# Four-layer cross attention, batches taken three at a time: another order of turns for the grouped-query layer, which adds into its input's tile

## The chip, the cores and the metric

The kernel runs on one core of one Trainium2 chip. The metric is the device time of one execution in microseconds. The profile is one execution taken by the hardware profiler; its engines are TensorE (PE, with weight loads shown apart as PEld), VectorE (DVE), ScalarE (ACT), GpSimd (POOL) and SyncE (SP, which here only issues DMAs).

## The reference

`x` is (4 batches, 512 queries, 256 channels); the context is (4, 1024 keys, 512 channels). Four cross-attention layers follow each other, and each one's output is the next one's input. All is float32.

```python
# layers 0, 2, 3: "masked", 16 heads of 64
q, k, v = x @ Wq, ctx @ Wk, ctx @ Wv
logits = q k^T * 64**-0.5 + col_bias      # col_bias: -20 * (1 - mask) in four chosen key columns
x = softmax(logits) v @ Wo + bo + x

# layer 1: grouped query, 16 query heads of 16, 4 key/value heads
xn = x * rsqrt(mean(x*x) + eps) * norm_w
q, k, v = xn @ wq, ctx @ wk, ctx @ wv
x = x + softmax(q k^T / 4) v @ wo
```

Batches do not depend on each other; layers of one batch do.

## The kernel before, in words

**Units.** Each layer of a batch is cut into eight units, so there are 4 x 4 x 8 = 128: 96 masked and 32 grouped. A masked unit is two heads of 64, side by side in the 128 partitions. A grouped unit is two heads as well, each in a stripe of 32 rows (16 and padding), with even and odd key blocks in the two halves of the partitions, so that four matmuls of 32 rows lie side by side; two consecutive units share one query projection and one output projection.

**Steps.** Two strings, `MASKED_TURNS` and `GROUPED_TURNS` (lines 55 to 62), say for each step which stream gives its next masked unit and which its next grouped unit; a dot is none. `order()` (line 65) pops the units. Before, stream 0 is batch 0 and then batch 2, stream 1 is batch 1 and then batch 3, and there are 104 steps: 72 with a masked unit alone, 24 with both ("attached"), and 8 with a grouped unit alone (steps 11 to 14, 28, 29, 78 and 79). The program is written out in this order by hand; each engine runs its own instructions in it.

**A step** (the loop at line 967) with a masked unit `g`, a grouped unit `lam`, the previous masked unit `g1` and the next step's grouped unit `coming`:

- `scores(g)` (line 642 on): 32 matmuls (line 652), ScalarE copies each 128x1024 tile out of PSUM (662), VectorE keeps a running maximum (666).
- The previous masked unit is attended, `attend(g1)` (684). If `lam` is there, its logits are computed again in four pairs between quarters of this (616) and ScalarE takes exponentials right out of PSUM (639).
- VectorE subtracts the maximum (749), ScalarE exponentiates (755), POOL adds up the running sums (794). These are interleaved by the due times in `events`.
- A list `fill` holds the TensorE work that needs no softmax: output projections of units attended a step earlier (840, added by VectorE at 862 or 858), query projections (548), `attend` of `lam`, keys of the masked unit two steps on (472), at the head of a grouped layer its keys (490) and RMS norm (580 to 595), then transposes of newly loaded inputs (378, 352), and values for the next step (514). Maxima of `coming` (608, logits at 616) are strewn between these by due time (line 1089).
- In a step with a grouped unit alone there are no scores, subtractions or running sums; maxima of `coming` and exponentials of `lam` alternate pair by pair (lines 1051 to 1063), with one output and one query projection in between.

**Buffers.** PSUM's eight banks are handed out by `Place`, longest free first. The states of the batches (a layer's input and the sum that becomes its output) live in four slots of one SBUF tile, `x_all`, given out and taken back by `new_state` and `drop_state`. Three contexts fit at once (`bufs=3`). The tile `stage` (one buffer) takes raw context and input as they are loaded, the norm's scratch and the rows to be stored. Keys, values, `xn` and query weights of the grouped layer have one buffer each.

**Loads.** SP's queue loads weights a few steps ahead. Raw context comes by POOL's gathers in four parts and x in a fifth, one a step, from five steps before the unit two ahead of a batch's first masked unit (lines 917 to 927). For batches 2 and 3 the fifth part is put off until the batch that gave them its stream is nearly done.

**project_out** (line 832): the first projection of a layer opens the next state. It takes a slot and writes input plus projection into it; later ones add in place. A grouped layer's input is dropped as soon as its first projection is added.

Of the kernel before, what the change touches and what calls it, by code (L numbers as in the profile page):

```python
# [17 lines left out]
B, S, C = 4, 512, 256  # L18
# [24 lines left out]
def units(b):  # L43
    out = []
    for l in range(4):
        for u in range(8):
            out.append(
                Group(l=l, b=b, u=u, p=u, r=u // 2, h=u % 2, first=u == 0, last=u == 7)
            )
    return out  # L50

MASKED_TURNS = (
    "00000000111....1111100000000..0011111111000000000000"
    "00111111111111111100000000..001111111100000011111111"
)
GROUPED_TURNS = (
    "...........00000000....11111111....................."  # L60
    ".....00000000........11111111......................."
)


def order():
    streams = [units(0) + units(2), units(1) + units(3)]
    steps = []
    for turns in zip(MASKED_TURNS, GROUPED_TURNS):
        steps.append([None if s == "." else streams[int(s)].pop(0) for s in turns])
        assert all(g is None or g.masked == (n == 0) for n, g in enumerate(steps[-1]))  # L70
    assert not any(streams)
    return steps


# [1 line left out]
def kernel(ctx: ExitStack, tc: tile.TileContext, a: dict, out: bass.AP):  # L76
# [240 lines left out]
    xs, ctx_t = {}, {}  # L317
# [3 lines left out]
    x_free, x_at = [0, 1, 2, 3], {}  # L321

    def new_state(l, b):
        x_at[l, b] = x_free.pop(0)
        xs[l, b] = x_all[:, x_at[l, b]]
        return xs[l, b]

    def drop_state(l, b):
        x_free.append(x_at[l, b])
# [246 lines left out]
    turns = []  # L576
# [255 lines left out]
    def project_out(g):  # L832
        x, acc = xs[g.l, g.b], xs.get((g.l + 1, g.b))
        opens = acc is None
        if opens:
            acc = new_state(g.l + 1, g.b)
        w = Place()
        m = w.ap
        for k in range(KC):
            nc.tensor.matmul(  # L840
                m[:, k * S : (k + 1) * S], lhsT=g.wo[:, k * P : (k + 1) * P], rhs=g.ot,
                start=True, stop=True,
            )
        y = m.rearrange("p (k q) -> p k q", q=S)

        def add_last(q):
            nc.vector.tensor_tensor(acc[:, :, q], y[:, :, q], acc[:, :, q], ALU.add)

        def add():
            if g is masked[-1]:  # L850
                for i in range(0, NI, 2):
                    add_last(slice(i * P, (i + 2) * P))
                    store(g.b, range(i, i + 2))
                left[g.b] = -1
            elif opens and g.masked:
                bo = columns[f"L{g.l}_xattn_bo"]
                for k in range(KC):
                    nc.vector.scalar_tensor_tensor(
                        acc[:, k, :], y[:, k, :], bo[:, k : k + 1], x[:, k, :], ALU.add, ALU.add
                    )  # L860
            else:
                nc.vector.tensor_tensor(acc, y, x if opens else acc, ALU.add)
            if opens and not g.masked:
                drop_state(g.l, g.b)
            w.back()

        left[g.b] -= 1
        return add

    def store(b, blocks=range(NI)):  # L870
        x = xs[4, b]
        o = t_([P, NI, C], "stage", f"out{b}_{blocks[0]}")
        w = Place()
        m = w.ap
        for n, i in enumerate(blocks):
            for k in range(KC):
                nc.tensor.transpose(
                    m[:, n * C + k * P : n * C + (k + 1) * P], x[:, k, i * P : (i + 1) * P], ident
                )
        count = len(blocks)  # L880
        (nc.vector.tensor_copy if blocks[0] else nc.scalar.copy)(
            o[:, 0:count, :], m[:, 0 : count * C].rearrange("p (i c) -> p i c", c=C)
        )
        if blocks[-1] == NI - 1:
            drop_state(4, b)
        w.back()
        nc.sync.dma_start(
            out=out[b].rearrange("(i p) c -> p i c", p=P)[:, blocks[0] : blocks[-1] + 1, :],
            in_=o[:, 0:count, :],
        )  # L890
# [3 lines left out]


    steps = order()
    masked = [g for g, _ in steps if g]
    step_of = {(g.l, g.b, g.u): n for n, both in enumerate(steps) for g in both if g}
# [3 lines left out]
    def at(n):  # L902
        return steps[n] if 0 <= n < len(steps) else (None, None)
# [14 lines left out]
    for b in range(B):  # L918
        first = next(g for g in masked if (g.b, g.l, g.u) == (b, 0, 0))
        for n, part_of in enumerate(load_parts(b, first.n == 0)):  # L920
            at_step = -1
            if first.n:
                before = masked[first.n - 2]
                at_step = step_of[before.l, before.b, before.u] - 5 + n
                if n == 4 and b > 1:
                    at_step = step_of[3, b - 2, 7] - 1
            parts.setdefault(at_step, []).append(part_of)

    def run(items):
# [37 lines left out]
    for n in range(len(steps) + 2):  # L967
        g, lam = at(n)
# [79 lines left out]
        if lam:  # L1048
            if g1:
                reciprocal_sums(g1)  # L1050
            for i in range(NT // 2):
                if g1:
                    attend(g1, range(2 * i, 2 * i + 2))
                if coming and not g:
                    pair(i)
                exponentials_pair(lam, i)
                if i == 0 and g:
                    g.mx_place.back()
                if not g:
                    if i == 1 and outs:  # L1060
                        project_out(outs.pop(0))()
                    if i == 2 and queries:
                        project_q(queries.pop(0))()
# [5 lines left out]
        elif g1 and g:  # L1069
            attend(g1)  # L1070
            if not ending:
                late.append(lambda: normalise(g1))
        elif g1:
            attend_last(g1)
            adds = [project_out(each) for each in outs]
            outs = []
            reciprocal_rows(g1.ot, g1.psum, g1.mx)
            scale_out(g1)
            for add in adds:
                add()  # L1080
# [10 lines left out]


        fill = [(1.8, lambda each=each: project_out(each)) for each in outs]
        outs = []
        of_queries = [(1.7, lambda each=each: project_q(each)) for each in queries]
# [97 lines left out]
```

## Time and profile before

| | |
|---|---|
| time, median of 3 runs (lowest to highest) | 3808.96 us (3808.76 to 3809.16) |
| the profiled execution's own time | 3809.19 us |
| its span, first to last instruction | 3807.4 us |
| granted TensorE clock, mean | 0.997 |
| PE busy | 3741.1 us (98%) |
| DVE busy | 3001.7 us (79%) |
| ACT busy | 2101.8 us (55%) |
| POOL busy | 1624.5 us (43%) |
| first matmul of the masked scores | 35.0 us after the span's start |

Busy time is a share of the whole span. Matmuls are pipelined and their ends are modelled, so a busy PE need not be PE at its peak. In the views of instructions a row is: start, duration, engine, line, operation, output<-inputs, shapes, count, and in brackets the idle time before it with what ended it. In views of stretches the columns are: start and end of the stretch, its length, then busy time and count of instructions for PE, PEld, DVE, ACT and POOL (for one line's instructions, of the engines it uses), the granted clock, the DMA engines' share and GB/s.

### The profile page before, as it was taken

What the parts mean: (1) busy time and instruction counts of PE and PEld (TensorE: products, weight loads), DVE (VectorE), ACT (ScalarE), POOL (GpSimd) and SP (SyncE); (2) the same over time, 40 slices, a digit from 0 to 9 for tenths busy, and PEclk for the clock granted to TensorE, in tenths of its full rate; (3) what the DMA queues carried; (4) which work ended last, traced back from release to release, by engine and by line L of the source; (5) the groups of instructions that cost most, each with busy time, mean ns of one, the idle gap of its engine ahead of it and who ended that gap; (6) DMA issues with size and microseconds to landing.
All of it is one profiled execution on the core that took longest, in us unless ns stands there. A gap on an engine that the chain in (4) does not pass through costs nothing.

```text
span 3807.4 us, 50450 instructions
## 1 busy us (share of the span) xinstructions
PE 3741.1 (98%) x19662; PEld 1879.9 (49%) x19662; DVE 3001.7 (79%) x3928; ACT 2101.8 (55%) x2433; POOL 1624.5 (43%) x749
## 2 busy tenths in 40 slices
PE   8999999999999999999999999999999999999998
PEld 4555444554434555555545444555444355555554
DVE  6887778778877888888887887788787778888887
ACT  4555455555545555555555555555555455555554
POOL 3555113443313555555553333445332155555554
PEclk9999999999999999999999999999999999999999
DMA  2111000010000001101011010100100000000100
GB/s 67 42 31 26 12 24 18 17 33 22 19 11 23 26 26 42 37 26 31 26 25 36 27 27 18 29 26 19 28 20 23 11 25 26 25 26 26 31 24 7
DMA packets 187874, 98.71 MB, mean 26 GB/s; under 512 B 43240, under 2 KB 183528, under 8 KB 187636
## 3 DMA queue, kind: packets, MB, share of 16 engines
q1 hardware_dynamic: 182510, 82.90, 7.9%
q0 software_dynamic: 2560, 8.39, 0.8%
q10 hardware_dynamic: 2566, 4.20, 0.5%
q8 instruction: 155, 2.54, 0.3%
q14 instruction: 83, 0.68, 0.1%
HBM read 89.16 MB, written 2.10 MB: 24 GB/s over the span
## 4 chain that ended last, share of the span: by engine, by line
PE 87%; DVE 8%; ACT 2%; issue 2%; DMA 0%; POOL 0%; DVEq 0%; ACTq 0%; POOLq 0%
PE ps L514 19%; PE ps L684 19%; PE ps L472 17%; PE ps L652 13%; PE ps L616 7%; PE ps L840 5%; PE ps L548 5%; DVE ps L666 4%; ACT st L662 1%; DVE st L749 1%; DVE st L608 1%; PE ps L490 1%; PE ps L658 1%; DVE qt L634 1%; PE ps L704 0%
## 5 line engine op out<-in xcount | busy, mean ns | idle before, releaser
L794 POOL TENSOR_TENSOR st<-st 128x1024 f32<-128x1024 f32 x668 | 1579.7, 2365 | 2059.7 <-ACT st L755 2015.7
L666 DVE TENSOR_TENSOR ps<-ps,st 128x1024 f32<-128x1024 f32 x672 | 828.2, 1232 | 466.3 <-ACT st L662 407.4
L755 ACT ACTIVATE st<-st 128x1024 f32<-128x1024 f32 x768 | 783.2, 1054 | 707.1 <-DVE st L749 695.2
L749 DVE TENSOR_TENSOR st<-st,ps 128x1024 f32<-128x1024 f32 x768 | 885.0, 1212 | 3.3
L684 PE MATMUL ps<-st,v 128*64 128x512 f32 (+1 forms) x4064 | 805.7, 597 | 0.5 <-DVE st L608 0.5
L662 ACT COPY st<-ps 128x1024 f32<-128x1024 f32 x768 | 715.4, 1047 | 101.8 <-PE ps L658 81.4
L514 PEld LDWEIGHTS ps<-wv,ctx 128*128 128x128 f32 x6400 | 729.8, 192 | 73.9 <-issue 63.6
L514 PE MATMUL ps<-wv,ctx 128*128 128x128 f32 x6400 | 742.3, 276 | 0.6 <-ACT st L662 0.6
L652 PE MATMUL ps<-qt,kt 64*128 64x512 f32 x3072 | 708.3, 598 | 1.4 <-ACT qt L554 1.4
L472 PE MATMUL ps<-ctx,wk 128*128 128x512 f32 x1536 | 689.6, 598 | 2.2 <-ACT ctx L384 2.2
L684 PEld LDWEIGHTS ps<-st,v 128*64 128x64 f32 (+1 forms) x4064 | 233.5, 130 | 545.6 <-issue 480.7
L472 PEld LDWEIGHTS ps<-ctx,wk 128*128 128x128 f32 x1536 | 288.1, 191 | 389.1 <-issue 373.2
L652 PEld LDWEIGHTS ps<-qt,kt 64*128 64x128 f32 x3072 | 283.8, 186 | 326.4 <-ACT st L662 146.0
L526 ACT COPY v<-ps 128x512 f32<-128x512 f32 x200 | 117.1, 585 | 497.1 <-PE ps L514 493.2
L608 DVE TENSOR_TENSOR st<-st,ps 128x1024 f32<-128x1024 f32 x224 | 273.3, 1220 | 129.8 <-PE ps L616 61.2
L616 PE MATMUL ps<-qt,kt 32*128 32x512 f32 x2048 | 323.8, 645 | 28.1 <-DVE qt L634 16.3
L639 ACT ACTIVATE st<-ps 128x1024 f32<-128x1024 f32 x256 | 248.4, 1023 | 185.2 <-PE ps L616 156.7
L840 PE MATMUL ps<-ot,wo 128*128 128x512 f32 x448 | 217.4, 611 | 1.4 <-DVE ot L829 0.7
L616 PEld LDWEIGHTS ps<-qt,kt 32*128 32x128 f32 x2048 | 103.4, 186 | 214.1 <-issue 57.1
L548 PE MATMUL ps<-x,wq 128*128 128x512 f32 x384 | 185.6, 606 | 1.8 <-ACT x L356 1.1
L477 ACT COPY kt<-ps 128x512 f32<-128x512 f32 x192 | 109.8, 572 | 77.3 <-PE ps L472 77.0
L840 PEld LDWEIGHTS ps<-ot,wo 128*128 128x128 f32 x448 | 78.5, 189 | 135.2 <-issue 124.2
(143 smaller groups left out, 1633.2 us busy)
## 6 DMA issues: line engine op xcount, KB each, us to landing
wk<-in_L_xattn_Wk_dram SPq DMA_DIRECT2D x96, 256.0 KB
wv<-in_L_xattn_Wv_dram SPq DMA_DIRECT2D x96, 256.0 KB
wq<-in_L_xattn_Wq_dram SPq DMA_DIRECT2D x96, 128.0 KB
wo<-in_L_xattn_Wo_dram SPq DMA_DIRECT2D x96, 128.0 KB
qt<-qt ACTq DMA_DIRECT2D x32, 128.0 KB
xraw<-in_x_dram SPq DMA_DIRECT2D x3, 512.0 KB
out_dram<-out SPq DMA_DIRECT2D x3, 512.0 KB
wq<-in_L_xattn_wq_dram SPq DMA_DIRECT2D x32, 32.0 KB
```

The lines of the kernel that those rows point to most:

```text
L472: nc.tensor.matmul(m, lhsT=g.wk[:, k, :], rhs=ctx_t[g.b][:, k, n * 512 : (n + 1) * 512], start=(k == 0), stop=(k == KT - 1),)
L514: nc.tensor.matmul(m[:, t * P : (t + 1) * P], lhsT=ctx_t[g.b][:, k, (4 * n + t) * P : (4 * n + t + 1) * P], rhs=g.wv[:, k, :], start=(k == ...
L548: nc.tensor.matmul(m, lhsT=g.wq[:, k, :], rhs=x[:, k, :], start=(k == 0), stop=(k == KC - 1))
L616: nc.tensor.matmul(ws[odd].ap[:, j * S : (j + 1) * S], lhsT=g.kt[rows, i * P : (i + 1) * P], rhs=g.qt[rows, :], start=True, stop=True,)
L652: nc.tensor.matmul(m[:, j * S : (j + 1) * S], lhsT=g.kt[g.rows[j], keys], rhs=g.qt[g.rows[j], :], start=True, stop=t > 0,)
L662: nc.scalar.copy(g.st[t], m)
L666: nc.vector.tensor_tensor(top, top, g.st[t], ALU.max)
L684: nc.tensor.matmul(g.po[at, :], lhsT=g.v[:, t, rows], rhs=g.st[t][:, j * S : (j + 1) * S], start=(t == first), stop=(t == last),)
L749: nc.vector.tensor_tensor(g.st[t], g.st[t], g.mb, ALU.subtract)
L755: nc.scalar.activation(st, st, AF.Exp)
L794: nc.gpsimd.tensor_tensor(g.acc, g.st[0] if t == 1 else g.acc, g.st[t], ALU.add)
L840: nc.tensor.matmul(m[:, k * S : (k + 1) * S], lhsT=g.wo[:, k * P : (k + 1) * P], rhs=g.ot, start=True, stop=True,)
```

## The change

Each batch becomes a stream of its own. The strings are new: 96 steps, each with a masked unit, and all 32 grouped units attached: batch 0's in steps 11 to 18, batch 1's in 21 to 28, batch 2's in 31 to 38, batch 3's in 67 to 74. Batches 0, 1 and 2 start their first layers one after the other (steps 0, 8, 16) and are in progress together; batch 3 starts at step 56, after batch 0 has ended at 47. The first projection of a grouped layer no longer opens a slot: the sum goes into the input's own tile, which becomes the next state under its own slot, and nothing is dropped. The exception for the fifth part of batches 2 and 3 is gone: x is loaded in the step after the last context part.

```diff
 MASKED_TURNS = (
-    "00000000111....1111100000000..0011111111000000000000"
-    "00111111111111111100000000..001111111100000011111111"
+    "000000001111111122222222000000001111111100000000"
+    "222222223333333311111111222233333333222233333333"
 )
 GROUPED_TURNS = (
-    "...........00000000....11111111....................."
-    ".....00000000........11111111......................."
+    "...........00000000..11111111..22222222........."
+    "...................33333333....................."
 )
...
-    streams = [units(0) + units(2), units(1) + units(3)]
+    batches = [units(b) for b in range(B)]
...
     def project_out(g):
         x, acc = xs[g.l, g.b], xs.get((g.l + 1, g.b))
         opens = acc is None
-        if opens:
+        if opens and g.masked:
             acc = new_state(g.l + 1, g.b)
+        elif opens:
+
+            acc = xs[g.l + 1, g.b] = x
+            x_at[g.l + 1, g.b] = x_at[g.l, g.b]
...
-            if opens and not g.masked:
-                drop_state(g.l, g.b)
...
                 at_step = step_of[before.l, before.b, before.u] - 5 + n
-                if n == 4 and b > 1:
-                    at_step = step_of[3, b - 2, 7] - 1
```

More of the change, by code (lines that the diff above doesn't have):

```diff
@@ L55 @@
 MASKED_TURNS = (
-    "00000000111....1111100000000..0011111111000000000000"
-    "00111111111111111100000000..001111111100000011111111"
+    "000000001111111122222222000000001111111100000000"
+    "222222223333333311111111222233333333222233333333"
 )
 GROUPED_TURNS = (
-    "...........00000000....11111111....................."
-    ".....00000000........11111111......................."
+    "...........00000000..11111111..22222222........."
+    "...................33333333....................."
 )
 def order():
-    streams = [units(0) + units(2), units(1) + units(3)]
+    batches = [units(b) for b in range(B)]
     steps = []
     for turns in zip(MASKED_TURNS, GROUPED_TURNS):
-        steps.append([None if s == "." else streams[int(s)].pop(0) for s in turns])
+        steps.append([None if s == "." else batches[int(s)].pop(0) for s in turns])
         assert all(g is None or g.masked == (n == 0) for n, g in enumerate(steps[-1]))
-    assert not any(streams)
+    assert not any(batches)
     return steps
```

## The prediction

> **What bounds the kernel now.** I read the page's busy shares first, then the chain that ended last, then cut the trace into steps and read stretches of it, and last the order of time inside one stretch.
>
> ```profile
> span 3807.4 us, 50450 instructions
> ...
> PE 3741.1 (98%) x19662; PEld 1879.9 (49%) x19662; DVE 3001.7 (79%) x3928; ACT 2101.8 (55%) x2433; POOL 1624.5 (43%) x749
> ...
> PE 87%; DVE 8%; ACT 2%; issue 2%; DMA 0%; POOL 0%; DVEq 0%; ACTq 0%; POOLq 0%
> ```
>
> TensorE is busy nearly all the time and carries 87% of the chain; 8% lies on VectorE. DMA is nowhere on it. The change leaves TensorE's work as it is, so the question is where TensorE loses time now, and 98% cannot tell: the ends of matmuls are modelled.
>
> So I cut by steps. Each masked step opens with the 32 score matmuls of line 652; the first of them marks its start. A step with a masked group alone lasts 31.94 us, again and again; with eight transposes in it, 32.82. In the next view the columns are start and end, length, and the busy time and count of each engine. The rows are: eight plain steps; three steps with transposes; the stretches that hold the grouped layer of batch 0 (steps 9 to 19), 1 (21 to 30), 2 (55 to 65) and 3 (71 to 80); the four grouped-only steps 11 to 14 alone; one attached step (62).
>
> ```profile
> 3286.85:3542.38 255.53, 255.53 (x1233) 136.54 (x1232) 210.97 (x272) 144.09 (x168) 132.74 (x57) 1.00 0.09 25
> 136.78:235.24 98.46, 98.46 (x489) 53.69 (x488) 79.39 (x102) 56.81 (x66) 53.65 (x26) 1.00 0.14 41
> 331.02:727.74 396.72, 383.92 (x2243) 177.70 (x2242) 297.39 (x384) 212.84 (x245) 120.69 (x61) 0.99 0.08 21
> 759.68:1187.65 427.97, 416.31 (x2397) 191.35 (x2396) 321.08 (x414) 231.46 (x267) 140.06 (x69) 0.99 0.09 21
> 1959.55:2477.10 517.55, 511.43 (x2909) 242.46 (x2908) 402.27 (x521) 291.31 (x335) 194.51 (x97) 1.00 0.11 28
> 2636.80:3063.20 426.40, 414.26 (x2398) 189.96 (x2397) 321.06 (x414) 231.48 (x267) 140.05 (x69) 1.00 0.09 21
> 418.90:507.24 88.34, 81.89 (x573) 28.85 (x572) 58.00 (x78) 41.15 (x46) 0.88 (x3) 1.00 0.08 18
> 2301.77:2350.11 48.34, 47.92 (x285) 21.42 (x284) 37.96 (x48) 28.16 (x32) 16.58 (x7) 1.00 0.06 17
> ```
>
> TensorE never idles in a plain step (255.53 busy of 255.53). In the grouped stretches it idles 12.8, 11.7, 6.1 and 12.1 us. The low one is batch 2, the only one whose eight grouped units all ride on masked steps. The four lone units alone idle 6.45 us, and POOL has 0.88 us of work there.
>
> The same stretches for the grouped logits (line 616, 512 matmuls in each):
>
> ```profile
> 331.02:727.74 396.72, 84.49 (x512) 28.36 (x512) 0.99 0.08 21
> 759.68:1187.65 427.97, 82.62 (x512) 26.69 (x512) 0.99 0.09 21
> 1959.55:2477.10 517.55, 75.78 (x512) 22.89 (x512) 1.00 0.11 28
> 2636.80:3063.20 426.40, 80.87 (x512) 25.51 (x512) 1.00 0.09 21
> ```
>
> One and the same work takes 5.1 to 8.7 us longer where part of it runs alone: part of a wait looks busy. The order of time inside a lone step shows which wait:
>
> ```profile
> 434.51 1.99 PE L616 MATMUL ps<-qt,kt 32*128 32x512 f32 x12
> 435.74 2.57 DVE L608 TENSOR_TENSOR st<-st,ps 128x1024 f32<-128x1024 f32 x2 [1.77 <-PE ps L616]
> ...
> 437.01 1.13 PE L616 MATMUL ps<-qt,kt 32*128 32x512 f32 x4 [0.52 <-DVE st L608]
> ```
>
> Maxima and exponentials of a lone unit take their PSUM places from each other; TensorE waits for VectorE to empty one (0.52 us here), while VectorE waited 1.77 us for TensorE. In attached steps eight such matmuls stand between attends or key projections (1.14 us each time at 2284.4, 2287.4 and 2290.4), and the emptying is covered.
>
> **What the Trainium skill says.** "TensorEngine Tiling (Array Packing)", PSUM Bottleneck: tiling speeds up the matmuls but not the emptying of PSUM, which may become the bottleneck. The trace agrees: eight packed matmuls, 1.14 us, make two 128x1024 tiles that VectorE takes 1.22 us each to fold in. "Perfetto Trace Analysis", Optimization Strategy: where the contended engine changes over time, interleaving the regimes may help. Plain steps (all TensorE) and lone steps (a ring of waits) are two such regimes. The same page, Identifying the Most-Contended Engine, says matmul busy time is no measure of distance from the roofline; the 84.49 against 75.78 agrees, so I sum lengths of steps, not busy times.
>
> **The change, part by part.**
>
> *Order of turns.* 104 steps become 96; 96 masked and 32 grouped units stay. Lone grouped steps go from 8 to 0, attached from 24 to 32. Of each stretch I take its length less 31.94 for each masked step in it, which is the price of one batch's grouped layer:
>
> - batch 0: 396.72 - 7 x 31.94 = 173.14 (four lone steps)
> - batch 1: 427.97 - 8 x 31.94 = 172.45 (two lone)
> - batch 3: 426.40 - 8 x 31.94 = 170.88 (two lone)
> - batch 2: 517.55 - 11 x 31.94 = 166.21; it also holds five eight-transpose parts of batch 3's load and a store's eight, at 32.82 - 31.94 = 0.88 each, 5.28: 160.93 (none lone)
>
> Before: 173.14 + 172.45 + 160.93 + 170.88 = 677.40. After: 4 x 160.93 = 643.72. Gain 33.7 us. Two lone steps cost nearly as much as four, so the loss belongs to the stretch with its way in and out: step 30, attached but with no masked group to attend, takes 39.30 us for 216 matmuls where step 64 takes 43.32 for 252, although the 36 missing (32 attends at 7.09, four projections at 1.7) are worth 8.8. All three stretches go, way in and out included.
>
> Cross-check: idle above batch 2's, 6.7 + 5.6 + 6.0 = 18.3, plus line 616 above batch 2's, 8.7 + 6.8 + 5.1 = 20.6, is 38.9, an upper end; it forgets that in attached steps other lines swell a little. I take the lengths.
>
> *What the new order moves past each other.* Batches 0 and 3 repeat batch 2's pattern with a four-step lead from the layer before. Batches 1 and 2 start two steps after the one before them ends, so steps 19 and 29 hold both a tail (one more output projection: 33.66 - 31.94 = 1.72) and a head (keys and norm: 42.68 - 31.94 = 10.74). The trace has no such step. Both are TensorE work and I add them: 44.40, nothing extra. Its cost lies between -1.7 each (the head's norm waits 1.73 us for ScalarE's square, which 1.72 us of matmuls ahead of it could cover) and +3.6 each: VectorE does 0.72 + 0.25 + 0.71 + 0.69 for the tail's sums and 1.22 for the second add ahead of subtractions, and the square stands behind the exponentials that wait for those. I take 0. Single buffers (keys, values, xn, query weights of the grouped layer) have their last reader in step 18 or before and are refilled from 19 on: cover one step.
>
> *Loads.* Parts of batch 2 fall in steps 9 to 13 and of batch 3 in 49 to 53, the same count as before, 0.88 each. x now comes right behind the context on SP's queue, ahead of that step's weights. Batch 1's did so up to step 5, steps 2 to 5 at 32.82 each: nothing. Store of batch 0 falls in step 49 and takes the staging tile between two context parts; POOL's gather of step 50 waits for that store. The last half store is issued at 3804.2 and all ends at 3807.4, so a whole one lands within some 6 us, and POOL is busy with running sums until 6.2 us into a step anyway (1953.58 + 12.11 against 1959.55). Running sums queue behind it, with about 10 us before they start. I take 0; uncovered it is 6 us, once.
>
> *In place.* The first add of a grouped layer writes onto its input. Same instruction and shape as the others of line 862 (1217 ns). Its other readers, the square and the norm's two multiplications in step 9, end four steps earlier: no wait, 0. It frees the fourth slot, which three batches at a time need.
>
> Sum: 3807.40 - 33.68 = 3773.72 span; 3809.19 - 3807.40 = 1.79 around it; 3775.5. The profiled execution is 0.2 above the median of the runs, so 3775.3.
>
> **Rivals.**
>
> 1. *As summed*, 3775.3; own range 3771 to 3780. For it: batch 2 is a measured copy of the end state. Chance 0.70.
> 2. *Head on tail costs*: steps 19 and 29 lose 3.6 each, 7, and the store's 6 us is not covered: 3788 at most, 3783 likely. Against it: VectorE has 42 us of work in a 50.8 us attached step, 29.5 in a head step. 0.12.
> 3. *More gain*: the cross-check's 38.9, or the cover of both norm waits (3.5): 3770. 0.10.
> 4. *No change*: the loss belongs to the layer's own chain and comes back spread over attached steps, 33.7 / 8 = 4.2 us on each of eight newly attached: 3809. Against it: batch 2's steps are 16.4 to 18.9 above a plain one, all eight. 0.05.
> 5. *Slower*: POOL. In the lone steps of batch 0 its memset of query weights (line 434) waited 67.6 us in two waits for a projection. If such a wait moves in front of the running sums (16.6 us a step), which the next step's row sums need some 15 us in while POOL ends at 6, all beyond 9 us stalls VectorE, its subtractions, then TensorE. It decides beyond 34 us over three heads, 11 each, hence waits of 20: 3815 at 22. Against it: in batch 2's attached steps the memset waits for nothing. 0.03.
>
> **How the numbers follow.** Forecast 3775.3. The range holds 1, 3 and most of 2: 3768 to 3786. About 0.2%, 7.6 us, is what a measurement can tell: faster 0.92, same 0.05, slower 0.03.
>
> **What would show it.** Attached steps at 48 to 51 us; every grouped stretch about 161 above 31.94 per masked step; line 616 near 4 x 75.8 = 303 us where it is now 323.8; TensorE's idle down from 66 to about 48 us; steps 19 and 29 near 44.4. Wrong if a step between 19 and 31 or 49 and 51 idles on TensorE for more than 3 us, if POOL waits on line 434 inside attached steps, or if line 616 stays at 324.

## The result, and the profile after

The changed kernel takes 3774.36 us (median; 3773.92 to 3774.68) against 3808.86 us for the kernel before in the same comparison: a ratio of 0.9911, 95% interval 0.9895 to 0.9926. The forecast was 3775.3. The profiled execution took 3773.92 us.

The page of the changed kernel, its lines for span, TensorE and the chain:

```profile
span 3772.2 us, 50461 instructions
...
PE 3723.8 (99%) x19662; PEld 1860.2 (49%) x19662; DVE 3000.4 (80%) x3928; ACT 2104.1 (56%) x2433; POOL 1625.0 (43%) x749
...
PE 86%; DVE 9%; issue 2%; ACT 2%; DMA 0%; DVEq 0%; POOL 0%; ACTq 0%; POOLq 0%
```

The 19662 matmuls are the same; TensorE's idle time went from 66.3 to 48.4 us and its busy time from 3741.1 to 3723.8. Line numbers are about one higher than before up to the projection (616 is now 617, 652 is 653), and five higher at the additions.

Stretches of the changed kernel. The rows are: eight plain steps (76 to 83); steps 9 to 39 with the grouped layers of batches 0, 1 and 2; steps 65 to 75 with that of batch 3; the two steps that hold a tail and a head (19 and 29); one attached step (23). Columns as before: stretch, length, busy time and count of PE, PEld, DVE, ACT and POOL, clock, DMA share, GB/s.

```profile
3124.53:3380.07 255.54, 255.54 (x1234) 136.49 (x1233) 211.18 (x273) 144.23 (x168) 130.79 (x56) 1.00 0.09 25
329.89:1807.42 1477.53, 1459.25 (x8307) 681.69 (x8307) 1153.90 (x1493) 825.50 (x950) 531.99 (x257) 1.00 0.09 23
2611.41:3124.53 513.12, 507.12 (x2868) 238.09 (x2867) 402.33 (x521) 286.44 (x330) 186.87 (x89) 1.00 0.09 23
813.56:857.95 44.39, 42.66 (x195) 20.70 (x194) 32.98 (x44) 21.83 (x25) 16.59 (x8) 1.00 0.11 23
1293.67:1338.06 44.39, 42.66 (x195) 20.71 (x194) 32.97 (x44) 21.83 (x25) 16.60 (x8) 1.00 0.12 23
1002.89:1053.72 50.83, 50.49 (x291) 22.39 (x291) 41.93 (x56) 27.91 (x32) 16.84 (x8) 1.00 0.08 23
```

The plain step has not moved: 255.54 / 8 = 31.94. Three grouped layers cost 1477.53 - 31 x 31.94 = 487.39, less five parts of a load at 0.88, 482.99: 161.0 each. The fourth costs 513.12 - 11 x 31.94 - 0.88 (a store) = 160.90. Together 643.9 where before they cost 677.4: 33.5 us of the 35.2 by which the span is shorter. The rest is the start (first scores at 33.8 instead of 35.0 us) and the last step (45.7 us from its first score matmul to the span's end, instead of 46.4), which the change does not explain. In the traces of all fourteen kernels of this document the first scores lie between 33.7 and 35.3 us, and the last step takes 45.7 us where the granted TensorE clock falls to half once in it and 46.2 to 47.8 us where it falls twice.

The grouped logits in the same two stretches:

```profile
329.89:1807.42 1477.53, 227.01 (x1536) 68.28 (x1536) 1.00 0.09 23
2611.41:3124.53 513.12, 75.64 (x512) 22.74 (x512) 1.00 0.09 23
```

302.65 us for all four, 75.7 for each: the price that only batch 2 had before.

What TensorE still waits for in the changed kernel, its own waits, longest first (total, times, longest):

```profile
PE ps L617 <- DVE qt L635: 12.8, 32, 0.7
PE ps L588 <- ACT xn L581: 6.9, 4, 1.7
```

The first is a wait before the first pair of exponentials in each of the 32 attached steps, for the queries that VectorE lowers by the maxima (line 635, "the lowering" from here on); the second is the norm's, once in each grouped layer.

### The profile page after: what moved, and what is told of

It is laid out like the page before. It is cut to its first block, busy times and chain, and to the rows that moved or that the text cites. A ratio compares the mean times of both kernels' runs of the same rounds, so it can differ in the third digit from the quotient of the medians.

```text
span 3772.2 us, 50461 instructions
## 1 busy us (share of the span) xinstructions
PE 3723.8 (99%) x19662; PEld 1860.2 (49%) x19662; DVE 3000.4 (80%) x3928; ACT 2104.1 (56%) x2433; POOL 1625.0 (43%) x749
## 4 chain that ended last, share of the span: by engine, by line
PE 86%; DVE 9%; issue 2%; ACT 2%; DMA 0%; DVEq 0%; POOL 0%; ACTq 0%; POOLq 0%
PE ps L515 19%; PE ps L685 18%; PE ps L473 17%; PE ps L653 12%; PE ps L617 7%; DVE ps L667 6%; PE ps L845 5%; PE ps L549 5%; ACT st L663 2%; DVE st L750 1%; PE ps L491 1%; DVE qt L635 1%; PE ps L659 1%; PE ps L705 0%; PE ps L379 0%
## 5 line engine op out<-in xcount | busy, mean ns | idle before, releaser
L685 PE MATMUL ps<-st,v 128*64 128x512 f32 x4064 | 810.9, 598 | 0.0
L685 PEld LDWEIGHTS ps<-st,v 128*64 128x64 f32 x4064 | 231.2, 130 | 551.5 <-issue 491.6
L617 PE MATMUL ps<-qt,kt 32*128 32x512 f32 x2048 | 302.6, 639 | 16.1 <-DVE qt L635 12.8
L617 PEld LDWEIGHTS ps<-qt,kt 32*128 32x128 f32 x2048 | 91.0, 183 | 191.0 <-ACT st L640 52.2
```

Of the source, the lines that this page charges most:

```text
L617: nc.tensor.matmul(ws[odd].ap[:, j * S : (j + 1) * S], lhsT=g.kt[rows, i * P : (i + 1) * P], rhs=g.qt[rows, :], start=True, stop=True,)
L685: nc.tensor.matmul(g.po[at, :], lhsT=g.v[:, t, rows], rhs=g.st[t][:, j * S : (j + 1) * S], start=(t == first), stop=(t == last),)
```

## Experiments

A lone step is one with a grouped unit alone, a break is one or more of them in a row, and the way in and the way out are the steps on either side. My theory: the 33.7 us are the three stretches with lone steps; they go with the stretch and not with each lone step in it, because in a lone step VectorE and TensorE take PSUM places from each other in a ring; the shared tile costs and brings nothing. Rivals: the shared tile matters; ScalarE's exponentials are the wait; every lone step has its own price.

**1. Each part alone.** The old order with the sum in the input's tile:

```diff
# kernel before
-        if opens:
+        if opens and g.masked:
             acc = new_state(g.l + 1, g.b)
+        elif opens:
+            acc = xs[g.l + 1, g.b] = x
+            x_at[g.l + 1, g.b] = x_at[g.l, g.b]
...
-            if opens and not g.masked:
-                drop_state(g.l, g.b)
```

> The old order of turns, with the grouped layer adding into its input's tile. My theory: the same instructions in the same order, so no change: 3808.9 within 2 us, the three stretches with lone grouped steps keep their 172.5, 173.1 and 170.9 us above 31.94 per masked step. Rival (the shared tile is what brings time, or costs a wait): more than 4 us either way, and VectorE's first add of the grouped layer (line 862 of before) waits longer.

Measured 3808.92 us, 1.0001 of the kernel before (0.9992 to 1.0009). The three stretches cost 173.3, 172.5 and 170.9 above their plain steps.

The new order, with a new state for batches 0 to 2:

```diff
# changed kernel
-        if opens and g.masked:
+        moves = opens and not g.masked and g.b < 3
+        if opens and (g.masked or moves):
             acc = new_state(g.l + 1, g.b)
...
                 nc.vector.tensor_tensor(acc, y, x if opens else acc, ALU.add)
+            if moves:
+                drop_state(g.l, g.b)
```

> The new order of turns, while batches 0, 1 and 2 open a new state in the grouped layer as before (batch 3 must stay in place, four slots don't hold it otherwise). My theory: the order brings everything, 3774.4 within 2 us. Rival (the shared tile brings a part): some 3/4 of that part comes back, over 3778.

Measured 3775.17 us, 0.9912 (0.9896 to 0.9929), and the grouped stretches as long as with the whole change (487.41 and 161.78 above the plain steps). So the order brings the gain, and the shared tile has no time of its own that these runs can tell. By the program's count of states, batch 3 alone needs it: when its grouped layer gives its first sum, in step 69, batch 1 holds two of the four slots, batch 2 one and batch 3's input one. There it is a condition of the order.

**2. Whose emptying is it?** Both kernels are the one before, with a smaller operation in lone steps only.

```diff
# small_fold: maxima of `coming` when there is no masked unit
-                nc.vector.tensor_tensor(g.mx, g.mx, w.ap, ALU.max)
+                nc.vector.tensor_tensor(few(g.mx), few(g.mx), few(w.ap), ALU.max)
# small_exp: exponentials of `lam` when there is no masked unit
-            nc.scalar.activation(g.st[2 * i + odd], w.ap, AF.Exp)
+            nc.scalar.activation(few(g.st[2 * i + odd]), few(w.ap), AF.Exp)
# few: 8 of each bank's 512 columns
```

> The kernel before, where in grouped-only steps VectorE folds only 16 of the 1024 columns of a logits tile into the maximum, so that PSUM is emptied sooner (the maxima are then incomplete: that part is left out). My theory: VectorE's emptying is the wait of lone steps, so 15 to 30 us go, to 3780 to 3794, and line 616 falls from 323.8 towards 303 us. Rival (the loss belongs to ScalarE's exponentials, or to the chain from maxima to query weights): less than 6 us.

> The kernel before, where in grouped-only steps ScalarE takes exponentials of only 16 of the 1024 columns of a tile (the other exponentials are left out). My theory: VectorE is the later of the two, so less than 8 us go, 3801 or more. Rival (ScalarE's emptying is the wait): 15 to 30 us go.

Small folds: 3792.47 us (one run, and one for small exponentials), 16.3 less than the kernel before. Its four grouped stretches (batches 0 to 3, the same steps as in the prediction's view):

```profile
331.13:721.49 390.36, 379.49 (x2243) 176.73 (x2242) 268.01 (x384) 212.42 (x245) 120.64 (x61) 1.00 0.09 21
753.44:1175.62 422.18, 411.91 (x2398) 190.11 (x2397) 306.43 (x414) 231.16 (x267) 140.06 (x69) 1.00 0.09 21
1947.49:2465.06 517.57, 511.44 (x2908) 242.33 (x2907) 402.35 (x521) 291.34 (x335) 194.50 (x97) 1.00 0.11 28
2624.77:3046.59 421.82, 411.92 (x2398) 190.13 (x2397) 306.45 (x414) 231.15 (x267) 140.04 (x69) 1.00 0.09 21
```

Above the plain steps these are 166.78, 166.66, 166.23 (with its loads and store, as before) and 166.30. From batches 0, 1 and 3, 6.3 + 5.8 + 4.6 = 16.7 us have gone, and 5.9, 5.7 and 5.4 us above 160.9 remain. The same place in a lone step as the prediction showed, in order of time:

```profile
433.25 2.58 PE L619 MATMUL ps<-qt,kt 32*128 32x512 f32 x16
434.48 0.47 DVE L611 TENSOR_TENSOR st<-st,ps 128x16 f32<-128x16 f32 x2 [1.77 <-PE ps L619]
...
435.77 1.98 PE L548 MATMUL ps<-xn,wq 128*128 128x512 f32 x4
```

Sixteen matmuls stand in a row, without the 0.52 us in the middle, and the two folds take 0.47 us instead of 2.57. Small exponentials: 3808.66 us, and the stretches at 172.93, 172.47, 166.24 and 170.89, each within 0.2 us of before.

So making VectorE's folds small takes half of the loss, and making ScalarE's exponentials small in lone steps takes none of it while the folds are whole. No run makes both small; with small folds, TensorE's visible waits for ScalarE in batch 3's two lone steps come to 0.3 us. Line 616 fell by 10.6 us only, to 313.2 and not towards 303. The other half is one price for each stretch, 5.4 to 5.9 us, for four lone steps as for two. The way out holds much of it: step 80, attached but with nothing to attend between its pairs of exponentials, takes 38.08 us in the kernel before and with small folds, 3.6 more than step 64 less its 36 missing matmuls (43.32 - 8.8). What TensorE waits for there, with small folds (the third line ends at the step's first matmul):

```profile
PE ps L619 <- DVE qt L637: 2.1, 1, 2.1
PE ps L548 <- ACT st L642: 0.7, 1, 0.7
PE ps L655 <- ACT qt L554: 0.7, 1, 0.7
PE ps L619 <- ACT st L642: 0.3, 1, 0.3
```

The longest is for the lowered queries (line 637 here), 2.1 us where an attached step of the changed kernel waits some 0.4; the second and fourth are for ScalarE's exponentials of an attached step, which neither run made small.

The granted TensorE clock has a small part too. In the kernel before it is at half for 6.83 us in step 15 and again in step 30, on the way out of the first two stretches, and at full speed in step 80, on the way out of the third. The two pieces at half speed, then steps 30 and 80:

```profile
519.00:525.83 6.83, 6.83 (x28) 2.93 (x24) 4.85 (x9) 6.32 (x7) 0.00 (x0) 0.50 0.01 2
1160.71:1167.54 6.83, 6.65 (x23) 3.17 (x22) 4.91 (x9) 6.43 (x8) 0.00 (x0) 0.50 0.00 0
1148.37:1187.66 39.29, 37.04 (x216) 19.50 (x216) 22.44 (x24) 26.27 (x30) 15.11 (x7) 0.91 0.09 28
3025.12:3063.20 38.08, 34.98 (x217) 18.14 (x217) 22.44 (x24) 26.16 (x30) 15.12 (x7) 1.00 0.10 28
```

With small folds neither step has such a piece; step 30 then takes 38.08 us as well, 1.2 less, and step 15 takes 45.74 instead of 46.67. So about 2.1 of the 16.7 us came by way of the clock, which leaves 14.6 for the waits at the folds themselves. Why the clock fell in these two steps and not in step 80 is not shown. The changed kernel's clock is at full speed from its first scores to its last step.

**3. How does it grow with the number of lone steps?** Dots put into the second half of the changed kernel's masked turns, where batch 3's grouped units ride:

```diff
# changed kernel; GROUPED_TURNS lengthened to match
-    "222222223333333311111111222233333333222233333333"
+    "22222222333333331111111.1222233333333222233333333"      # lone_one
+    "22222222333333331111111..1222233333333222233333333"     # lone_two
+    "222222223333333311111....111222233333333222233333333"   # lone_four
+    "222222223333333311111.11.1222233333333222233333333"     # lone_apart
```

> The changed kernel with one grouped-only step put into batch 3's grouped layer (its fifth unit). My theory: the loss belongs to a stretch with its way in and out: about 9 us above the changed kernel, 3783. Rival (a loss for each lone step, 3.0 to 5.8 us from the stretches of before): 3778 to 3780.

> The changed kernel with two grouped-only steps, one after the other, in batch 3's grouped layer (fifth and sixth unit). Both theories: about 10 us above the changed kernel, 3784, since before had two stretches of this length at 10.0 and 11.5 us above the attached batch.

> The changed kernel with four grouped-only steps in a row in batch 3's grouped layer (third to sixth unit). My theory: 11 to 13 us above the changed kernel, 3786 to 3787.5. Rival (a loss for each lone step): 20 us, 3794.

> The changed kernel with two grouped-only steps apart from each other in batch 3's grouped layer (third and sixth unit). My theory: two stretches, so twice what one lone step costs, about 18 us above the changed kernel, 3792. Rival (a loss for each lone step): as much as two in a row, 10 us, 3784.

Times: 3794.30, 3794.95, 3794.62 and 3802.62 us, one run each, so I go by the stretch that holds the same 14 masked steps from the layer's head on. One line for each kernel, in this order: changed kernel, lone_one, lone_two, lone_four, lone_apart.

```profile
2611.41:3220.35 608.94, 602.95 (x3329) 289.27 (x3328) 481.64 (x624) 340.53 (x393) 234.67 (x109) 1.00 0.09 24
```

```profile
2612.64:3238.50 625.86, 609.78 (x3329) 293.30 (x3329) 482.17 (x624) 340.84 (x393) 234.73 (x109) 0.99 0.09 23
```

```profile
2612.39:3240.21 627.82, 609.22 (x3330) 294.27 (x3329) 482.34 (x624) 340.45 (x393) 234.60 (x109) 0.99 0.09 23
```

```profile
2611.55:3240.67 629.12, 609.28 (x3330) 297.32 (x3329) 482.76 (x624) 340.03 (x393) 234.49 (x109) 0.99 0.09 23
```

```profile
2612.70:3248.51 635.81, 613.26 (x3329) 295.41 (x3328) 482.49 (x624) 340.67 (x393) 234.59 (x109) 0.99 0.09 23
```

The work is the same, and the lengths differ by +16.9, +18.9, +20.2 and +26.9 us. One lone step costs nearly what four in a row do, so the price is for breaking the rhythm in the main. The rival's prices per lone step fit only the four: 3.0 to 5.8 us expected for one and 16.9 measured, 10 for two apart and 26.9 measured, 20 for four and 20.2 measured. But my sizes were wrong as well, each by 7 to 9 us: 9 expected for one, 10 for two, 11 to 13 for four, 18 for two apart.

Two apart would be 33.8 at twice one. To see what each break cost, I cut both kernels at the step between them. First the changed kernel, the steps with batch 3's second to fourth unit (68 to 70) and those with its fifth to eighth (71 to 74, with a store); then lone_apart, the same units with one lone step in each part and without the store:

```profile
2750.87:2898.39 147.52, 146.34 (x860) 65.20 (x859) 117.90 (x151) 84.30 (x96) 50.50 (x24) 1.00 0.08 21
2898.39:3090.87 192.48, 190.92 (x1122) 86.57 (x1121) 149.66 (x196) 111.01 (x126) 66.76 (x30) 1.00 0.08 22
2752.15:2885.49 133.34, 122.79 (x710) 52.94 (x709) 93.15 (x118) 66.56 (x75) 33.91 (x17) 0.96 0.07 17
2885.49:3054.03 168.54, 159.78 (x955) 70.34 (x954) 122.33 (x160) 91.88 (x104) 48.75 (x23) 1.00 0.06 17
```

Each part of lone_apart has one masked step less. The break at the third unit costs 133.34 - (147.52 - 31.94) = 17.8 us, that at the sixth 168.54 - (192.48 - 31.94 - 0.88) = 8.9. In the kernel before, two lone steps at the sixth and seventh unit cost 11.5 and 10.0, and four from the first unit on 12.2. So breaks that begin at the third or fifth unit cost 17 to 20 us, those at the first or sixth 9 to 12. TensorE's longest waits in lone_one from step 70 on:

```profile
PE ps L630 <- DVE mcol L730: 3.0, 1, 3.0
PE ps L617 <- DVE qt L635: 2.8, 2, 2.4
PE ps L617 <- DVE short L815: 2.1, 1, 2.1
```

All are for VectorE: on the way in for the column maxima (3.0), in the lone step for the sums of the masked unit (2.1), on the way out for the lowered queries (2.4). In lone_apart the first two are 3.0 and 2.0 at the third unit and 1.2 and 0.6 at the sixth, 3.3 us of the difference of 8.9. An odd-numbered unit comes right after a pair of units is finished, whose normalising (lines 571 to 800) stands on VectorE ahead of those sums. The clock differs too: at the third unit it is at half for 3.41 and 6.83 us, which is worth 5.1 us at most (an estimate, half of 10.24), and at the sixth it is at full speed. lone_one has the same two pieces, lone_two and lone_four two of 3.41 us. No run holds the clock still or leaves out the finished pair, so how the rest of the 8.9 us divides is not shown.

**4. Can the remaining waits be taken too?** Three kernels on top of the changed one: the lowering of the grouped queries two score tiles earlier; the norm behind the next unit's values; both.

```diff
# lower_early (also in both)
-            if t == 5:
+            if t == 3:
                 within()
# norm_late (also in both): the whole of norm(), square and matmuls
-            fill.append((1.7, norm))                 # ahead of loads and values
+            fill.append((1.7, norm))                 # behind values(masked[g.n + 1])
```

> The changed kernel with the lowering of the grouped queries after the fourth score tile of the step instead of after the sixth. In the changed kernel TensorE waits 12.8 us in all for it (line 617 for VectorE's line 635), about 0.4 in each attached step. My theory: that wait goes and nothing takes its place: 3762, 10 to 13 us less. Rival (the pair is then held up by PSUM places or by ScalarE, which empties the last score tiles until then): less than 3 us.

> The changed kernel with the norm's matmuls behind the values of the next masked unit in the head step of a grouped layer, so that ScalarE's square is done by then. TensorE waits 1.73 us there, four times. My theory: 6 to 7 us less, 3768. Rival (the norm's reciprocals come later on VectorE and hold up the next step's subtractions or its query projection): no gain, or up to 5 us more.

> Both edits on the changed kernel. If each stands for itself: the sum of the two, 3755 to 3758. Rival (they share a resource): less than the larger of the two.

All three miss. lower_early: 3808.4 us (0.9999 of the kernel before, 0.9991 to 1.0007): the whole gain of the change is lost again. norm_late: 3780.08 us, 5.7 more than the changed kernel. Both: 3812.03. TensorE's waits with the lowering early:

```profile
PE ps L653 <- DVE qt L635: 39.1, 32, 1.5
PE ps L588 <- ACT xn L581: 6.9, 4, 1.7
```

The wait for line 635 is still there, three times as long, and it is now a score tile (653) that waits. In step 23 the matmuls for the lowering start at 1017.58 us, but VectorE reaches it only at 1020.94, behind three running maxima. The lowering holds its PSUM place until then, and the seventh score tile is next in turn for that place. The 32 attached steps grew by 1.03 us on average, 33.0 in all. With the norm late, TensorE still idles 1.63 us before line 588: the square moved along with its matmuls and stands on ScalarE's queue behind the copies of the very values that were put ahead of it (the last copy starts at 370.51 us, the square at 371.00). The norm's VectorE work now comes ahead of the next step's running maxima, which in step 10 start 4.2 us into the step instead of 3.4. The steps after three of the heads grew by 0.6 to 0.8 us; step 10 grew by 2.3, but in it the granted clock is also at half for 3.41 us.

With that known, a fourth kernel leaves the square and the lowering where they are, and puts TensorE work in front of what waits for them:

```diff
# changed kernel
-                    attend(g1, range(2 * i, 2 * i + 2))
+                    attend(g1, (range(0, 3), range(3, 5), range(5, 7), range(7, 8))[i])
...
-            fill.append((1.7, norm))                 # square and matmuls
+            fill.append((0.0, square))               # the square alone
...
-            fill += values(masked[g.n + 1])
+            of_v = values(masked[g.n + 1])
+            fill += of_v[:2] + late_norm + of_v[2:]  # the norm's matmuls
```

> The changed kernel with two edits that leave every PSUM place in its turn. In a head step the square of the norm is issued where it was, but the norm's matmuls stand behind the first half of the values; and in attached steps the masked unit's eight attended blocks stand three, two, two and one before the four pairs of exponentials, so that the first pair comes 0.9 us later. My theory: the head steps 9, 19, 29 and 65 lose their wait of 1.7 us each, and the 32 attached steps their 0.34 to 0.42 us, 6.8 + 12.8, and nothing takes their place: 3755, at most 3760. Rival (a wait that is taken away at one place comes back behind the next PSUM place or the next instruction in the queue, as with the lowering moved early and the norm moved late): no less than 3771. The steps of the trace tell the two edits apart.

3760.67 us (3759.14 to 3762.23), 0.9874 of the kernel before (0.9858 to 0.9891): 13.7 us under the changed kernel, the fastest version here. What TensorE waits for longest in it, and its group of grouped logits:

```profile
PE ps L188 <- DVE tok_f L185: 4.3, 1, 4.3
PE ps L379 <- DMA st<-in_ctx_dram,key_rows: 3.9, 4, 2.3
```

```profile
L617 PE MATMUL ps<-qt,kt 32*128 32x512 f32 x2048 | 310.2, 639 | 3.3 <-DVE ot L830 3.3
```

Both waits are gone, and only those of the start are left on top. The four head steps are shorter by 1.8 to 1.9 us each, 7.2 in all. The attached steps gave 7.4 us of the 12.8 expected (1557.2 to 1549.8 us for all 32). The other 5.4 are found in TensorE's busy time, which rose from 3723.8 to 3729.3 us for the same 19662 matmuls, line 617's by 7.6 (302.6 to 310.2): part of what was idle is now inside matmuls that look longer. So the expected 3755 was 6 us too low, and 3760, named as the most, was just missed.

## Why the prediction was right

- *Price of a batch's grouped layer.* Forecast 643.7 for four, measured 643.9. The 1.8 us at the start and in the last step, which no term foresaw, are why the span came out 1.5 us under the forecast 3773.7. Lengths of whole steps were the right measure; the cross-check by idle time and line 616, 38.9 us, would have been 5 too much, as taken.
- *Steps that the trace did not have.* Tail and head in one step: forecast 44.40, measured 44.39 twice. The head's wait of 1.73 was not covered and VectorE's extra work was not felt: rivals 2 and 3 do not happen.
- *Attached steps.* They take 48.3 to 51.6 us, as forecast, but for the last of each layer, 43.3 to 43.6. The prediction's "16.4 to 18.9 above a plain one, all eight" misread batch 2 in the same place: its eighth, step 64, takes 43.32 us, 11.4 above. Rival 4 (33.7 us spread over eight of them) is refuted by the stretches all the same.
- *POOL.* The memset of query weights waits for nothing in the changed kernel: it is not among POOL's waits at all. Rival 5 does not happen. The context parts in steps 49 to 53 cost their 0.88; steps 49 to 53 take 33.69, 32.82, 32.82, 32.82, 32.82 (49 holds a store as well), and step 54 32.11.
- *In place.* 0, as experiment 1 shows. But the statement that three batches at a time need the freed slot was too broad: batches 0 to 2 fit without it.
- *Idle and line 616.* Forecast 48 and 303 us, measured 48.4 and 302.6.
- *Why lone steps lose.* This was half right. The loss does belong in the main to the stretch (experiment 3), and VectorE's emptying of PSUM is in it (experiment 2), but with 16.7 of 33.7 us, 2.1 of these by way of the clock, of which the prediction has nothing. Its step 30 of 39.30 us, too, holds 1.2 us of clock. The other 17 us are 5.4 to 5.9 us for each break, of which the way out shows some 3.6. The forecast did not need this split, since it took the whole stretch; the number was right with a mechanism that covers half of the loss.

## What to carry to other kernels

Where a dominant engine runs steps of constant length, price a part by the length of a stretch less its constant steps: it holds idle time and hidden waits alike, and here it foretold the time to 1 us. A short break in an interleaved rhythm cost here by its way in and out more than by its length (16.9 us for one lone step, 20.2 for four), so try to remove whole breaks. Two waits of the changed kernel went when TensorE work was put in front of the waiting instruction and the producer stayed where it was. Issuing the producer earlier made one of them three times as long, because it held its PSUM place for longer; moving the producer back together with the waiting instruction left the other nearly as it was (1.63 us of 1.73). And look at the granted clock of each stretch before putting all of its length down to waits.

## What was not expected

- Four lone steps cost 20.2 us and one 16.9; where the break begins matters more, 17 to 20 at the third or fifth unit against 9 to 12 at the first or sixth.
- The granted clock was at half for 6.83 us on the way out of two of the three stretches of the kernel before, and not in any grouped layer of the changed kernel.
- A lowering issued two tiles earlier costs 33 us, as much as the whole change brought.
- Taking 12.8 us of visible idle time from TensorE shortened the attached steps by 7.4 us; the rest reappeared as TensorE busy time with the count of matmuls unchanged.
